# Choosing the tokens of eight experts: one search for all ahead of them, or one for the first and the others in steps between matmuls

## The chip, the cores and the metric

The kernel runs on one core of a Trainium2 chip. The metric is the device time of one execution in microseconds (us). Before the change it is 1625.28, the median of three runs from 1625.16 to 1626.9. Engines are named as in the profile: PE (TensorE matmul), PEld (its weight load), DVE (VectorE), ACT (ScalarE), POOL (GpSimd), SP (SyncE).

## The reference

The input is 4 rows of 1024 tokens with 256 values each, float32. Two layers follow, each an attention part and a feed-forward part around layer norms and residual sums. Only the last part matters here, a mixture of eight experts in which each expert chooses its tokens:

```python
n = b * l                                   # 4096 tokens
k = min(max(int(n * C / e), 1), n)          # 4096 * 2 / 8 = 1024 per expert
S = jax.nn.sigmoid(xt @ Wg).T               # scores, 8 x 4096
G, I = jax.lax.top_k(S, k)
ex = xt[I]
hid = jax.nn.gelu(jnp.einsum('ekh,ehf->ekf', ex, W1) + b1[:, None, :], approximate=False)
out = (jnp.einsum('ekf,efh->ekh', hid, W2) + b2[:, None, :]) * G[..., None]
new_x = jnp.zeros_like(xt).at[I.reshape(-1)].add(out.reshape(-1, h))
```

W1 is 8 x 256 x 1024 and W2 8 x 1024 x 256. A layer norm of new_x is added to the tokens at the end.

## The kernel before, in words

The tokens lie in SBUF in eight blocks of 512, each in four tiles of 128. The first layer runs block by block, the second layer's attention row by row; PE, DVE and ACT issue in the order in which the program is written (a hand-made schedule), POOL and SP in the order of the framework's scheduler. POOL too is ordered by hand from the seventh expert on.

**End of the attention.** For the last two tiles of 128 tokens, `close` returns the function `at_once` (L1249). It projects the attention output, adds the residual, does three layer norms one after the other on DVE with a `pow` on POOL in each, stores the normalized tokens in `tok_d` (L1190), transposes them (`turn_gating`, L1203) and computes their gate logits (`gate`, L1216), which it adds to the tile `logits` (L1233). `logits` has 128 partitions, one per pair of a token segment and an expert (16 segments of 256 tokens), and 256 columns. `keep_busy` (L203) issues matmuls whose result nobody reads.

**Search.** After that, in the stage that begins at L1434, `sc` becomes the sigmoid of all logits (L1468 to L1471). It is also transposed and stored beside the token rows, eight DMAs of 32-byte rows (L1486). Each expert's threshold, the 1024th largest score, is then found bit by bit for all experts at once: 15 rounds (L1497) of two bits. A round compares all scores with three values, each in an operation that also counts (L1501), adds up the counts over the 16 segments of the expert with a matmul by the 0/1 matrix `same_b` (L1505), and keeps the largest value with a count of at least 1024 (L1516, L1520). The next values to try are that value with two more bits (L1509).

**Lists.** From the threshold follow, for all experts in the same operations, a mask, the ties that still have room, the place of each chosen token in its expert's list (two scans, L1548 and L1552), a transpose to tokens, and the two halves of the place, `hi` (which chunk of 128) and `lo` (where in it), L1556 to L1564. What is left is done per expert by the class `List` (L1571): `chunks` and `places` build 0/1 matrices on DVE, `collect` multiplies them on PE in 32 small bf16 matmuls into the PSUM tile `parts`, ACT copies this to `listed`, and `gather` makes the token numbers `idx` with one more matmul and has POOL fetch eight chunks of 128 token rows from `tok_d` into `got` with indirect DMAs (L1628).

**Experts.** `feed_forward(u)` (L1805) does 512 tokens, half an expert; u runs from 0 to 15, two units (QPE = 2) per expert. Its first part has FC = 8 pairs of float32 matmuls `ph` (L1819), each followed by a Gelu on ACT; its second part has four output tiles of 128 tokens, `py` (L1842), which DVE scales and POOL adds to `acc_d` in DRAM with an indirect DMA (L1861). The tokens of the next unit are transposed on PE (`turn`, L1790) after the second and third output tile. Unit 0 does its first part in two halves of 256 tokens. While an expert's first unit runs, the next expert's `chunks` and `places` are issued among the ph matmuls, its four `collect` groups between ph and py, and its `gather` after the first output tile. Two sets of expert weights are loaded at a time, from SP.

Of the kernel before, what the change touches and what calls it, by code (L numbers as in the profile page):

```python
# [18 lines left out]
P = 128  # L19
D = 256  # L20
# [27 lines left out]
NROUND = 15  # L48
# [23 lines left out]
def kernel(  # L72
# [130 lines left out]
    def keep_busy(bank, n):  # L203

        for _ in range(n):
            nc.tensor.matmul(
                bank, lhsT=same_b, rhs=same_b.unsqueeze(1).to_broadcast([P, 4, P]), start=True, stop=True
            )
# [18 lines left out]
    with ExitStack() as st1:  # L227
# [183 lines left out]
        def later_counts():  # L411
            r = {}

            def count_int(name, shape, pattern, per_partition, tag=None):
                n_i = const.tile(shape, I32, tag=tag or name, name=name, bufs=3 if tag else 1)
                nc.gpsimd.iota(n_i, pattern=pattern, base=0, channel_multiplier=per_partition)
                return n_i

            def count(name, shape, pattern, per_partition, dtype):
                n_i = count_int(f"{name}_i", shape, pattern, per_partition, "whole")  # L420
                r[name] = const.tile(shape, dtype, name=name)
                nc.gpsimd.tensor_copy(r[name], n_i)
# [3 lines left out]
            count("count_p", [P, P], [[1, P]], 0, BF16)  # L426
            count("count_c", [P, NC], [[1, NC]], 0, BF16)
            count("count_t", [P, SEG // P, SEGB, B], [[1, SEG // P], [SEG // P, SEGB], [KT, B]], 0, BF16)
            r["count_t"] = r["count_t"].rearrange("p k z b -> p (k z b)")
            count("in_tile", [P, 1], [[0, 1]], 1, F32)  # L430
            r["row_i"] = count_int("row_i", [P, 1], [[0, 1]], 1)
            r["bits0"] = count_int("bits0", [P, 4], [[1, 4]], 0)
            r["expert_i"] = count_int("expert_i", [P, P], [[1, P]], -1, "whole")
            r["column_i"] = count_int("column_i", [P, P], [[1, P]], 0, "whole")
# [7 lines left out]
        def later_constants(r):  # L442
# [13 lines left out]


            def segment(name, n, p_i):

                row = const.tile([P, n], I32, tag="whole", name=f"{name}_row", bufs=3)  # L460
                nc.vector.tensor_scalar(row, p_i, 3, B - 1, ALU.logical_shift_right, ALU.bitwise_and)
                nc.vector.tensor_scalar(p_i, p_i, 5, None, ALU.logical_shift_right)
                n_f = const.tile([P, n], F32, name=name)
                nc.vector.scalar_tensor_tensor(n_f, row, float(SEGB), p_i, ALU.mult, ALU.add)
                return n_f

            expert_i = r["expert_i"]
            nc.vector.tensor_scalar(expert_i, expert_i, NE - 1, None, ALU.bitwise_and)

            same_b = const.tile([P, P], BF16, name="same_b")  # L470
            nc.vector.tensor_scalar(same_b, expert_i, 0.0, None, ALU.is_equal)
            earlier_b = const.tile([P, P], BF16, name="earlier_b")
            nc.vector.scalar_tensor_tensor(
                earlier_b, segment("seg_m", P, r["column_i"]), segment("seg_k", 1, r["row_i"]), same_b,
                ALU.is_gt, ALU.mult,
            )

            bits = const.tile([P, NROUND, 4], I32, name="bits")
            for n in range(NROUND):
                nc.vector.tensor_scalar(  # L480
                    bits[:, n, :], r["bits0"], 2 * (NROUND - 1 - n), None, ALU.logical_shift_left
                )

            counts = []
            for i in range(2):
                count_i = const.tile([P, 4], BF16, name=f"counts{i}")
                nc.vector.memset(count_i, float(SEG))
                counts.append(count_i)
# [4 lines left out]
            return mb1, strip, same_b, earlier_b, bits, counts, fold  # L493
# [468 lines left out]
        for t in range(NB):  # L962
# [6 lines left out]
            elif t == 1:  # L969
                mb1, strip, same_b, earlier_b, bits, counts, fold = later_constants(whole)  # L970
# [69 lines left out]
    spare = const.tile([P, 1], F32, name="spare")  # L1040
    with ExitStack() as st3:
# [96 lines left out]
        def close(t, h, oT, tiles, at_end):  # L1138
# [77 lines left out]
            def gate():  # L1216
# [15 lines left out]
                rows = slice(32 * (z0 + us[0]), 32 * (z0 + us[-1] + 1))  # L1232
                nc.vector.tensor_tensor(logits[rows, :], logits[rows, :], pg[rows, :], ALU.add)  # L1233
# [15 lines left out]
            def at_once(by_weight, back):  # L1249
# [7 lines left out]
                keep_busy(idle, 4)  # L1257
# [4 lines left out]
                keep_busy(idle, 34)  # L1262
                for i, pt in pts:
                    nc.vector.tensor_tensor(y[:, i, :], pt, h[:, i, :], ALU.add)
# [13 lines left out]
                gate()  # L1278
# [155 lines left out]
    with ExitStack() as st4:  # L1434
# [5 lines left out]
        parts = parts_ps.tile([P, P + NC], F32, name="parts")  # L1440
        nc.vector.memset(parts, 0.0)
# [14 lines left out]

        hi = keep.tile([P, NE, NTILE], BF16, name="hi")
        lo = keep.tile([P, NE, NTILE], BF16, name="lo")  # L1460
        each = keep.tile([P, P, NTILE], BF16, name="each")
        with ExitStack() as sa:
            wk = sa.enter_context(tc.tile_pool(name="gate", bufs=2))
            w1 = sa.enter_context(tc.tile_pool(name="pick", bufs=1))
            ps = sa.enter_context(tc.tile_pool(name="gate_ps", bufs=2, space=PSUM))

            sc = w1.tile([P, SEG], F32, name="sc")
            nc.vector.tensor_scalar(sc, logits, -87.0, None, ALU.max)  # L1468
            nc.scalar.activation(sc, sc, AF.Exp, scale=-1.0)
            nc.vector.tensor_scalar(sc, sc, 1.0, None, ALU.add)  # L1470
            nc.vector.reciprocal(sc, sc)  # L1471
            idle = ps.tile([P, TB], F32, tag="idle", name="idle", bufs=1)
            keep_busy(idle, 13)

            def by_token(src, name):
                pt = ps.tile([P, SEG // P, NSEG * NE], F32, tag="tp", name=name)
                for k in range(SEG // P):
                    nc.tensor.transpose(pt[:, k, :], src[:, k * P : (k + 1) * P], ident)
                return pt

            scores_t = w1.tile([P, SEG // P, SEGB, B, NE], F32, name="scores_t")
            nc.scalar.copy(scores_t.rearrange("p k z b e -> p k (z b e)"), by_token(sc, "scoreT"))
            rows_d = tok_d.rearrange("(b z k p) d -> k z p b d", b=B, z=SEGB, p=P)
            for k in range(SEG // P):
                for z in range(SEGB):
                    nc.sync.dma_start(rows_d[k, z][:, :, D : D + NE], scores_t[:, k, z])  # L1486
            nc.scalar.copy(each, count_p.unsqueeze(2).to_broadcast([P, P, NTILE]))

            nc.scalar.activation(spare, sc[:, 0:1], AF.Gelu)

            thr = w1.tile([P, 1], F32, name="thr")
            tried = bits[:, 0, :].bitcast(F32)
            for r in range(NROUND):  # L1497
                n = counts[r % 2]
                for k in range(1, 4):
                    ge = wk.tile([P, SEG], F32, tag="ge", name="ge")  # L1500
# [70 lines left out]
        class List:  # L1571


            def __init__(self, e):
                self.e, self.at = e, {}
# [351 lines left out]
```

## Time and profile before

| what | us |
|---|---|
| median of the runs | 1625.28 |
| profiled execution | 1625.33 |
| its span | 1623.5 |
| last attention product ends, about | 1075 |
| sigmoid done, first comparison | 1093.27 |
| threshold known, mask begins | 1122.99 |
| `hi`, `lo` ready, `which` begins | 1130.42 |
| `idx` of expert 0 begins | 1135.37 |
| first `ph` matmul | 1141.76 |
| last `py` matmul ends, about | 1613 |

Times of instructions are counted from the span's start. In a row of a timeline the first number is the start, the second the length, then the engine, the line, the operation, its output and inputs. A row with x32 stands for 32 instructions. In rows by stage the busy time of each engine follows the stretch and its length. A float32 matmul of the program shows as two PE instructions.

### The profile page before, as it was taken

To read this page: it belongs to the slowest core of one execution; us is meant where nothing else is said; L and a number is where in the kernel's file an instruction comes from. 1 tells how busy PE (TensorE), PEld (TensorE's weight loads), DVE (VectorE), ACT (ScalarE), POOL (GpSimd) and SP (SyncE) were. 2 spreads that over 40 slices of the span, in tenths; PEclk is the share of its full clock that TensorE was granted. 3 is DMA by queue.
4 is the path that set the end of the run, shared out by engine and by line. 5 is a ranking of instruction groups with operands and counts; after the bars stand their busy time and mean duration, and the time that the engine had idled before them with its cause. 6 is when DMAs were issued, how large, how long until landed. Compare 5 with 4: busy or idle time off the path is not lost.

```text
span 1623.5 us, 23583 instructions
## 1 busy us (share of the span) xinstructions
PE 1562.3 (96%) x9270; PEld 797.6 (49%) x9270; DVE 904.9 (56%) x2080; ACT 647.6 (40%) x1115; POOL 402.0 (25%) x436
## 2 busy tenths in 40 slices
PE   7999999999999999999999999983999999999997
PEld 3666666666322223232323224541757667566574
DVE  5555565664657787878787787767211212222145
ACT  3344444544544545454544455641221121211233
POOL 4122232222201011111101010110424324324555
PEclk9999999999999999999999999996999999999999
DMA  8300000000000000101010100031233233233355
GB/s 205 121 1 1 1 1 1 0 1 1 1 1 1 11 31 7 34 1 40 1 40 1 36 4 27 28 129 30 57 75 70 66 75 72 66 75 88 67 146 140
DMA packets 70090, 71.22 MB, mean 44 GB/s; under 512 B 23613, under 2 KB 62938, under 8 KB 69850
## 3 DMA queue, kind: packets, MB, share of 16 engines
q1 hardware_dynamic: 56096, 47.01, 9.4%
q0 software_dynamic: 13008, 21.77, 7.4%
q8 instruction: 73, 1.20, 0.3%
q10 hardware_dynamic: 874, 0.93, 0.2%
q14 instruction: 39, 0.32, 0.1%
HBM read 41.74 MB, written 27.95 MB: 43 GB/s over the span
## 4 chain that ended last, share of the span: by engine, by line
PE 92%; DVE 3%; issue 2%; POOL 1%; ACT 1%; DMA 0%; POOLq 0%; SPq 0%; ACTq 0%; DVEq 0%
PE sc L1303 17%; PE po L1329 16%; PE ph L1819 13%; PE py L1842 13%; PE py L799 4%; PE pg L691 4%; PE pv L707 3%; PE ph L855 2%; PE po L771 2%; PE pt L1145 2%; PE pv L380 2%; PE pq L356 2%; PE pq L876 2%; PE po L775 2%; PE pk L356 2%
## 5 line engine op out<-in xcount | busy, mean ns | idle before, releaser
L1312 ACT ACTIVATE w<-sc 128x512 f32<-128x512 f32 x512 | 277.9, 594 | 218.5 <-PE sc L1303 101.7
L1317 DVE TENSOR_SCALAR w<-sc 128x1024 f32<-128x1024 f32 x240 | 293.2, 1222 | 99.2 <-PE sc L1303 71.1
L1303 PE MATMUL sc<-qT,kT 32*128 32x512 f32 (+1 forms) x2304 | 294.7, 586 | 1.5 <-ACT w L1312 0.8
L1329 PE MATMUL po<-w,vaug 128*17 128x512 f32 (+1 forms) x2304 | 276.1, 550 | 1.0 <-ACT w L1315 0.3
L1842 PE MATMUL py<-w,hid 128*128 128x256 f32 x1024 | 230.1, 380 | 0.0
L1826 ACT ACTIVATE hid<-ph,mb 128x512 f32<-128x512 f32 (+1 forms) x136 | 90.1, 662 | 344.4 <-PE ph L1819 343.7
L1819 PE MATMUL ph<-xT,w 128*128 128x512 f32 (+1 forms) x544 | 222.8, 567 | 0.7 <-DVE xT L1803 0.7
L1842 PEld LDWEIGHTS py<-w,hid 128*128 128x128 f32 x1024 | 191.1, 190 | 32.0 <-issue 7.0
L1303 PEld LDWEIGHTS sc<-qT,kT 32*128 32x128 f32 x2304 | 94.4, 183 | 173.9 <-issue 157.9
L1819 PEld LDWEIGHTS ph<-xT,w 128*128 128x128 f32 x544 | 103.2, 190 | 111.1 <-issue 107.6
L1329 PEld LDWEIGHTS po<-w,vaug 128*17 128x17 f32 x2304 | 44.8, 95 | 191.5 <-issue 157.5
L1861 POOL DMA_INDIRECT acc_d<-y,idx x56 | 88.2, 1574 | 156.1 <-issue 127.0
L1628 POOL DMA_INDIRECT got<-tok_d,idx x64 | 65.9, 1030 | 152.3 <-DVE idx L1618 135.2
L1859 DVE TENSOR_TENSOR y<-py,mb 128x256 f32<-128x256 f32 x56 | 23.4, 419 | 142.3 <-PE py L1842 135.9
L1803 DVE COPY xT<-tp 128x512 f32<-128x512 f32 (+1 forms) x34 | 22.3, 660 | 91.6 <-PE tp L1798 91.6
L1067 POOL TENSOR_TENSOR rsg<-veg,mhalf 128x1 f32<-128x1 f32 x30 | 16.7, 555 | 205.0 <-DVE veg L1066 205.0
L691 PE MATMUL pg<-nT,wh 128*128 128x512 f32 x128 | 60.8, 607 | 1.5 <-ACT nT L630 1.5
L799 PE MATMUL py<-wo,oT 128*128 128x256 f32 x256 | 61.9, 385 | 0.0
L707 PE MATMUL pv<-wh,nT 128*128 128x512 f32 x128 | 59.7, 592 | 0.0
L1618 DVE CAST idx<-parts 128x8 int32<-128x8 f32 x8 | 1.3, 167 | 101.8 <-PE parts L1616 101.8
L799 PEld LDWEIGHTS py<-wo,oT 128*128 128x128 f32 x256 | 47.3, 190 | 17.2 <-issue 9.4
L572 POOL TENSOR_TENSOR x<-x,y 128x1024 f32<-128x1024 f32 x14 | 32.9, 2351 | 73.3 <-ACT y L561 73.3
(295 smaller groups left out, 1933.3 us busy)
## 6 DMA issues: line engine op xcount, KB each, us to landing
w<-in_L_ffn_W_dram SPq DMA_DIRECT2D x16, 1024.0 KB, 5.2
x<-in_L_attn_x_dram SPq DMA_DIRECT2D x8, 512.0 KB, 4.0
acc_d<-logits SPq DMA_DIRECT2D x8, 512.0 KB, 5.1
tok_d<-hg SPq DMA_DIRECT2D x32, 128.0 KB, 1.7
x_d<-x SPq DMA_DIRECT2D x7, 512.0 KB, 2.9
back_w<-acc_d SPq DMA_DIRECT2D x6, 512.0 KB
out_dram<-x SPq DMA_DIRECT2D x20, 128.0 KB, 1.7
out_dram<-back_w POOLq DMA_DIRECT2D x4, 512.0 KB
```

The costliest lines, as they stand in the source:

```text
L691: nc.tensor.matmul(pg, lhsT=wh[:, c, HID + e * P : HID + (e + 1) * P], rhs=d["nT"][:, c, :], start=(c == 0), stop=(c == DC - 1),)
L707: nc.tensor.matmul(pv, lhsT=d["nT"][:, c, i * P : (i + 1) * P], rhs=wh[:, c, 0:HID], start=(c == 0), stop=(c == DC - 1),)
L799: nc.tensor.matmul(py, lhsT=d["oT"][:, e, :], rhs=wo[:, e, :], start=(e == 0), stop=(e == EC - 1))
L1303: nc.tensor.matmul(sc[:, m * n : (m + 1) * n], lhsT=row["kT"][t][rows, r, (kt + m) * P : (kt + m + 1) * P], rhs=row["qT"][rows, t, q0 : q0 ...
L1312: nc.scalar.activation(w[:, j, :], sc, AF.Relu)
L1317: nc.vector.tensor_scalar(w[:, 2:4, :], pair, 0.0, None, ALU.max)
L1329: nc.tensor.matmul(po[32 * j : 32 * j + HD + 1, weighed(halves, r)], lhsT=row["v"][:, kt + m, HQ * t + 2 * j + r, :], rhs=w[:, j, m * n : ...
L1628: return nc.gpsimd.indirect_dma_start(out=dst, out_offset=None, in_=rows[:, :], in_offset=self.at_chunk(c), bounds_check=NT - 1, oob_is_er ...
L1819: nc.tensor.matmul(ph, lhsT=w1[:, c, f * P : (f + 1) * P], rhs=xT[u][:, c, h * n : (h + 1) * n], start=(c == 0), stop=(c == DC - 1),)
L1826: nc.scalar.activation(hid[:, f, h * n : (h + 1) * n], ph, AF.Gelu, bias=mb1[:, e * FC + f : e * FC + f + 1])
L1842: nc.tensor.matmul(py, lhsT=hid[:, f, i * P : (i + 1) * P], rhs=w2[:, f, :], start=(f == 0), stop=(f == FC - 1),)
L1861: scatter = nc.gpsimd.indirect_dma_start(out=acc_d[:, :], out_offset=lists[e].at_chunk(k), in_=y, in_offset=None, bounds_check=NT - 1, oob ...
```

## The change

The 15 rounds for all experts are replaced by `Search` objects: one for expert 0, one for expert 1, one for 2 and 3, one for 4 to 7. Scores now lie by tokens: `score_t` has 128 partitions (token in its tile) and 32 x 8 columns (tile, expert), in the memory of `logits`. A round takes three bits: seven values are compared with the expert's 32 columns in one `tensor_tensor` per expert, into a bf16 tile of 7 x 32, and one `tensor_reduce` adds up the 32. There are ten rounds. The matmul that adds up over partitions is by `all_b`, all ones. Only expert 0's search forms the next values for all outcomes ahead of the counts (`grown`); the others choose first and put the bits in afterwards.

Ranks are done per expert too (`sort`, `rank`), on 32 columns: two matmuls (by `all_b` and the triangular `upto_b`), two scans and some small operations.

Ahead of the experts stand expert 0's search and list. While its first rows are fetched, three steps of expert 1's search are issued. All other steps are in `agenda`, in order, each with a planned time and the first unit at which it may be issued. `go_on_with_lists` is called after every pair of ph matmuls, with 1.75 us (0.87 in unit 0), and after every output tile, with 2.3 us; it issues at most one step, when at most 0.3 us of the steps before are planned to be left.

`at_once` now transposes the logits that are known and computes their sigmoid and stores it beside its own chain; those of the last 256 tokens follow by themselves. Score stores to `tok_d` are two DMAs.

```diff
-NROUND = 15
+NBITS, NPER = 30, 3
+NVAL = 2**NPER
...
             def at_once(by_weight, back):
...
-                keep_busy(idle, 4)
+                tokens = side([P, SEG // P, P], "tokens")
+                for k in range(SEG // P):
+                    nc.tensor.transpose(tokens[:, k, :], logits[:, k * P : (k + 1) * P], ident)
+                keep_busy(idle, 3)
                 by_weight()
                 back()
...
+                for k in range(SEG // P):
+
+                    nc.vector.tensor_scalar(
+                        score_t.rearrange("p (b z k) e -> p k z b e", b=B, k=SEG // P)[:, k],
+                        tokens[:, k, :].rearrange("p (z b e) -> p z b e", b=B, e=NE),
+                        -87.0, None, ALU.max,
+                    )
+                known = score_t[:, 0 : NTILE - SEG // P]
+                nc.scalar.activation(known, known, AF.Exp, scale=-1.0)
...
                 turn_gating(tiles[0])
-                gate()
+                nc.vector.tensor_scalar(known, known, 1.0, None, ALU.add)
+                nc.vector.reciprocal(known, known)
+                score_rows = tok_d.rearrange("(j p) d -> p j d", p=P)[:, :, D : D + NE]
+                nc.sync.dma_start(score_rows[:, 0 : NTILE - SEG // P], known)
+
+                pg, rows = gate()
+                last_logits = wk.tile([P, SEG], F32, tag="y", name="last_logits")
+                nc.vector.tensor_copy(last_logits[rows, :], pg[rows, :])
+                tokens = side([P, SEG // P, 32], "tokens")
+                for k in range(SEG // P):
+                    nc.tensor.transpose(tokens[:, k, :], last_logits[rows, k * P : (k + 1) * P], ident[rows, rows])
+                new = score_t[:, NTILE - SEG // P : NTILE]
+                nc.vector.tensor_scalar(new, tokens[:, :, 32 - NE : 32], -87.0, None, ALU.max)
+                nc.scalar.activation(new, new, AF.Exp, scale=-1.0)
+                nc.vector.tensor_scalar(new, new, 1.0, None, ALU.add)
+                nc.vector.reciprocal(new, new)
+                nc.sync.dma_start(score_rows[:, NTILE - SEG // P : NTILE], new)
...
+            def compare(self, r):
+                g = len(self.es)
+                ge = wk.tile([P, NE // 2, NVAL - 1, NTILE], BF16, tag="ge", name="ge", bufs=1)
+                shape = [P, NVAL - 1, NTILE]
+                for i, e in enumerate(self.es):
+                    nc.vector.tensor_tensor(
+                        ge[:, i],
+                        score_t[:, :, e].unsqueeze(1).to_broadcast(shape),
+                        self.tried[:, i, 1:].unsqueeze(2).to_broadcast(shape),
+                        ALU.is_ge,
+                    )
+                with nc.allow_low_precision(reason="whole numbers up to 32"):
+                    nc.vector.tensor_reduce(self.counts[:, r % 2, :, 1:], ge[:, 0:g], AX.X, ALU.add)
+
+            def tick(self, r):
+
+                g, v = len(self.es), NVAL
+                pn = parts[:, sums_at : sums_at + g * v]
+                counts = self.counts[:, r % 2].rearrange("p g v -> p (g v)")
+                nc.tensor.matmul(pn, lhsT=all_b, rhs=counts, start=True, stop=True)
...
+                    if self.es == (0,):
...
+                        nc.vector.tensor_tensor(
+                            grown.bitcast(I32),
...
+                        nc.vector.scalar_tensor_tensor(
+                            kept, pn.to_broadcast([P, v, v]), float(TOPK), grown, ALU.is_ge, ALU.mult
+                        )
+                        nc.vector.tensor_reduce(tried[:, 0], kept, AX.X, ALU.max)
+                    else:
...
+                        nc.vector.scalar_tensor_tensor(kept, pn, float(TOPK), self.tried, ALU.is_ge, ALU.mult)
+                        best = wk.tile([P, g], F32, tag="best_g", name="best")
+                        nc.vector.tensor_reduce(best, kept, AX.X, ALU.max)
+                        nc.vector.tensor_tensor(
+                            tried.bitcast(I32),
+                            best.bitcast(I32).unsqueeze(2).to_broadcast([P, g, v]),
+                            now.unsqueeze(1).to_broadcast([P, g, v]),
+                            ALU.bitwise_or,
+                        )
+                    self.tried = tried
+                    self.compare(r + 1)
...
+            def steps(self, behind=0):
+
+                spent = 0.15 + 0.6 * len(self.es)
+                return [
+                    (spent, behind, lambda: self.compare(0)),
+                    *((spent + 0.85, behind, lambda r=r: self.tick(r)) for r in range(NBITS // NPER)),
+                ]
...
+            def rank(self):
+
+                for n, which in enumerate((all_b, upto_b)):
+                    nc.tensor.matmul(
+                        pre[:, n].rearrange("p v j -> p (v j)"),
+                        lhsT=which,
+                        rhs=self.kinds.rearrange("p v j -> p (v j)"),
+                        start=True,
+                        stop=True,
+                    )
...
+            def steps(self):
+
+                behind = max(QPE * self.e - 3, 0)
+                return [
+                    (0.5, behind, self.sort),
+                    (2.6, behind, self.rank),
+                    (1.2, behind, self.chunks),
+                    (1.4, behind, lambda: (self.places(0), self.places(1))),
+                    (1.4, behind, lambda: (self.places(2), self.collect(0), self.places(3), self.collect(1))),
+                    (0.3, behind, lambda: (self.collect(2), self.collect(3))),
+
+                    (0.3, behind + 1, self.gather),
+                ]
...
-                if not u:
+                if not u and not h:
                     for c in range(DC):
-                        turn(0, c, h)
+                        turn(0, c, 0)
                 for f in range(FC):
+                    if not u and not h and f in (FC - 4, FC - 3):
+                        turn(0, f - FC + 4, 1)
...
+                    if u or h or f not in (FC - 5, FC - 4, FC - 3):
+                        go_on_with_lists(u, 1.75 if u else 0.87)
...
-                if i == 0 and coming is not None:
-                    coming.gather()
-                if i in (1, 2) and u + 1 < NE * QPE:
+                if u == 1:
+                    if i == 2:
+                        for c in range(DC):
+                            turn(u + 1, c)
+                elif i in (1, 2) and u + 1 < NE * QPE:
                     turn(u + 1, i - 1)
...
+                go_on_with_lists(u, 2.3)
...
+        searches = [Search(0), Search(1), Search(2, 3), Search(4, 5, 6, 7)]
+        agenda = []
+        for search in searches[1:]:
+            agenda.extend(search.steps())
+            for e in search.es:
+                agenda.extend(lists[e].steps())
+        left = [0.0]
+
+        def go_on_with_lists(u, time):
+            left[0] = max(left[0] - time, 0.0)
+            if agenda and left[0] < 0.3 and agenda[0][1] <= u:
+                spent, _, step = agenda.pop(0)
+                left[0] += spent
+                step()
+
         first = ps.tile([P, TB], F32, tag="mm", name="idle", bufs=3)
-        keep_busy(first, 15)
+        for n, (_, _, step) in enumerate(searches[0].steps() + lists[0].steps()):
+            step()
+            if n == 0:
+                nc.vector.memset(parts[:, 0 : P + NC], 0.0)
+            if step == lists[0].rank:
+                keep_busy(first, 8)
+        for _ in range(3):
+            agenda.pop(0)[2]()
+            keep_busy(first, 4)
```

## The prediction

> **What bounds the kernel now.** I read the page's totals first, then the busy time by stage, then the chain of work and the instructions in order of time inside the one stage where TensorE isn't full.
>
> ```profile
> PE 1562.3 (96%) x9270; PEld 797.6 (49%) x9270; DVE 904.9 (56%) x2080; ACT 647.6 (40%) x1115; POOL 402.0 (25%) x436
> ...
> 1060.00:1110.00 50.00, 31.99 (x289) 15.96 (x281) 35.59 (x135) 17.40 (x25) 4.50 (x7) 0.87 0.42 130
> 1110.00:1150.00 40.00, 24.33 (x129) 13.59 (x130) 21.62 (x88) 4.71 (x10) 8.42 (x8) 0.78 0.10 28
> 1150.00:1200.00 50.00, 50.00 (x232) 36.85 (x232) 11.42 (x26) 9.56 (x17) 17.34 (x14) 1.00 0.26 56
> 1200.00:1300.00 100.00, 100.00 (x408) 64.17 (x407) 21.24 (x49) 19.79 (x30) 35.86 (x29) 1.00 0.33 71
> ```
>
> Columns after the stretch: its length, then busy us of PE, PEld, DVE, ACT, POOL, the granted clock, DMA. PE is the bound nearly everywhere, the experts' stage included (100.00 of 100.00, DVE at 21), but not between about 1075 and 1142 us. There VectorE and short round trips set the time. One of the 15 rounds of the search, from the chain that ended last:
>
> ```profile
> 1119.04 1.30 DVE ge L1501 x6
> 1120.34 0.05 issue
> 1120.38 0.20 PE pn L1505
> 1120.61 0.19 DVE kept L1516
> 1120.82 0.18 DVE tried L1520
> 1121.02 1.30 DVE ge L1501 x6
> ```
>
> The round repeats after 1.98 us (1119.04 to 1121.02): three compare-and-count passes in 1.30, a matmul of counts, two small VectorE steps. Two dependent VectorE steps stand 0.03 apart beyond their length. So whatever shortens this stage moves the end, and whatever adds PE work after 1142 moves it back.
>
> What PE pays for one small bf16 matmul between float32 ones shows at the list's gather matmul:
>
> ```profile
> 1187.43 7.07 PE L1842 MATMUL py<-w,hid 128*128 128x256 f32 x32
> ...
> 1217.89 3.72 PE L1842 MATMUL py<-w,hid 128*128 128x256 f32 x16
> 1221.45 0.17 PE L1616 MATMUL parts<-fold,listed 128*128 128x8 bf16 x1
> 1221.47 3.70 PE L1842 MATMUL py<-w,hid 128*128 128x256 f32 x16
> 1225.01 0.60 PE L1798 MATMUL tp<-ident,got 128*128 128x128 f32 x4
> ```
>
> Two py blocks with it: 1217.89 to 1225.01 = 7.12 us; without it 1187.43 to 1194.34 (the next transpose) = 6.91. So 0.21 us, though the matmul has 8 columns.
>
> **What the Trainium skill says.** "VectorE: DVE Perf Modes", the perf-mode tier table: float32 tensor_tensor and every tensor_reduce run at one element a cycle. The trace agrees for the first: x<-x,back_w of 128x1024 took 1.225 us and upto<-upto,mask of 128x256 0.42, so 1.05 ns an element and 0.152 fixed. For the reduce it has only 16 elements, 0.17 us. "TensorE: Matmul & The Clock Gate", Part 1: the array drops to half clock when idle and needs some 3.4 us of work to come back. Here the granted clock is 0.50 from 1098 to 1126, and 13 matmuls begun at 1124.01 bring it to 1.00 after 1127.4. "SBUF — State Buffer", Who interferes with whom: a VectorE instruction with two SBUF inputs contends with a GpSimd instruction that reads SBUF. Before, VectorE is idle during the first gather, so no row here shows it.
>
> **The change part by part.** The profiled execution took 1625.33 us, span 1623.5 and 1.8 around it; the median is 1625.28, the same within 0.1.
>
> *Scores.* Before, from the last logits add (1089.53) to the first comparison (1093.27): 3.74 us, 1.75 of it the reciprocal of 256 columns. After, all but the last two of the 32 token tiles are done earlier. Their two clamps lie in VectorE's 0.79 wait for pt (1077.07 to 1077.86; two 128-column PSUM reads, about 0.29 each), their add and reciprocal (0.28 + 1.65) in its 2.37 wait for pg (from 1087.2): cost nothing, with 0.2 to 0.4 to spare; without cover about 2.5. On the path stay a copy 0.43, two small transposes 0.25, clamp 0.17, exp 0.22, add 0.15, reciprocal of 16 columns 0.25 (den has that shape and time), and six gaps of 0.04: 1.7. **Gain 2.05.** The extra PE transposes stand where one filler matmul goes. SP's score stores change from 8 issues to 2 with the same 32-byte rows (6.3 us to land before); weights of 3 MB may stand before or behind them on that queue. DMA was quiet from 1104, and the first reader comes at about 1115, so neither order costs.
>
> *Search.* A round of the first expert: kept and its maximum over 64 elements, 0.22 each (0.17 for 16 elements, plus 48 more at 1.05 ns); the comparison 7x32 = 224 elements, 0.152 + 0.235 = 0.39; the sum over the same 224, 0.39; four gaps of 0.03, issue 0.05, matmul 0.20, gap 0.03: 1.62. The or of 64 integers fits in the matmul's wait. A strided read is no extra: lo<-part, 256 elements at such a stride, took 0.39. Ten rounds: nine of 1.62, the first comparison 0.85 and a last 0.7: 16.1 (15.5 to 17, the reduce being unseen at this size). Before: 1093.27 to 1122.99 = 29.7. **Gain 13.6.**
>
> *List of expert 0.* Before, thr to which: 1122.99 to 1130.42 = 7.4, over 256 columns and with transposes. After: two compares of 32 columns 0.3, matmul 0.3, two scans 0.4 (256 took 0.68), then nine steps of 0.15 to 0.22, two of them overlapping: about 2.8. **Gain 4.6.** From which to idx (5.1) and to the first ph (6.2) the operations stay. Three steps of expert 1's search go into the gather's wait: some 4.1 us of VectorE work in the 5.7 before the first xT copy, so no cost unless they slow POOL's descriptors (0 to 4, taken 0). ACT's each copy and Gelu table (3.6 + 1.3 in before, 1094 to 1099) come earlier and are over long before listed needs ACT at about 1114. The memset of parts, 0.17, moves into the first matmul's wait of 0.28: nothing, 0.17 uncovered. POOL's memsets of the counts are new; the queue is idle from 1086.4 and they are due at 1091.6: nothing, about 0.5 each (its shortest tensor steps take 0.26 to 0.55) if late. Eight fillers behind rank take 8 x 0.43 = 3.4 at half clock, over before the first collect is ready.
>
> *Start of expert 0.* The second half's transposes go between ph matmuls, so PE's 0.39 wait for xT at 1149.76 goes. **Gain 0.4.** Sum of gains 20.65.
>
> *What comes back.* Seven experts' searches and ranks now stand in PE's queue in the full stage. 3 x 10 counts less the 2 issued early = 28 matmuls; at 0.2 (from the 0.21 above) 5.6. Seven ranks of two matmuls, 0.3: 2.1. Collect in two groups where it was one: seven more interruptions, 1.4. **Cost 9.1.** The bounds are 0.1 apiece (a transpose amid py costs 0.11) and 0.3: 4.5 to 14.
>
> Does a count matmul wait for VectorE? Behind it are all ph and py. Walking the agenda: in the first unit a step goes every second slot, 2 x 0.87 of ph and 0.2; VectorE's chain for one expert is 3 x 0.2 + 0.85 and gaps, 1.6. For two experts 2.4 against 3.5 or more. For four experts the comparison is 4 x 0.39 and the sum 896 elements, 1.1; with the small steps 3.5 against 3.7. Just enough, so 0; if the chain is 20% slower, 0.5 on each of seven ticks, 3.5. All lists are out in unit 12, and list 1's gather in unit 1, 15 us ahead of its transposes, on a POOL queue that issues the first unit's scatters earlier. Y evictions wait behind a step for up to 3.5 us, with two py banks: no cost.
>
> Sum: -20.65 + 9.1 = -11.5 us. **1625.3 - 11.5 = 1613.8.** In L0 the constants change a few operations beside a full PE: nothing.
>
> **The rivals.**
> - *Cheap insertions*, 0.1 each: PE prefetches weights (PEld is 64% busy in the stage) and hides all but the matmul. 1625.3 - 20.65 + 4.5 = 1609. Against: the 0.21 is measured in this very place.
> - *Wait in place of wait.* VectorE's new work meets POOL's descriptors of the first gather (+3), the four-expert ticks hold PE (+3.5), or PE starts expert 0 at half clock (+2 to 3): one or two of them, about 1619. For it: the thin margin, 8 fillers instead of 25; against: DVE is 21% busy in the stage.
> - *Slower.* Each insertion drains PE's pipeline and holds the float32 weights behind it. Place: the 42 insertions counted above (28 counts, 7 rank pairs, 7 collect groups). From 20.65/42 = 0.49 us each nothing is left, from 0.57 it is slower by over 0.2%; at 0.7 it costs 29.4 and ends at 1634. For it: each comes alone, after a wait on VectorE's semaphore, which gather's doesn't test; against: gather's 0.21.
>
> **How the numbers follow.** Forecast 1613.8, chance 0.58 (1611 to 1617). Cheap insertions 0.22. Wait in place of wait 0.15, some of it within 0.2% of before (3.3 us, about what a measurement here can tell from no change). Slower 0.03, and 0.02 for what I don't see. Range 1608 to 1619.5. Faster by over 0.2% 0.93, within 0.04, slower 0.03.
>
> **What would show it.** Right: tried to tried 1.6 us; first comparison near 1091.2; threshold near 1107; first ph near 1121.5; first ph to the end some 9 us longer than before (481.8), with parts and pre rows of 0.2 each. Wrong: the new sum far above 0.39 us; PE waiting for DVE at the counts in the experts' stage; granted clock below 1.00 after the first ph; got fetches longer than 1.02 us.

## The result and the profile after

The changed kernel takes 1616.98 us, the median of five runs from 1616.53 to 1618.01; the kernel before, run beside it, 1625.49 (five runs, 1625.16 to 1626.9). The ratio is 0.9946, 95% interval 0.9932 to 0.9961: 8.5 us less, where 11.5 were forecast. The profiled execution is the slowest of the five: 1618.01 us, span 1616.2.

The same rows of totals and stages as before (columns: length, busy us of PE, PEld, DVE, ACT, POOL, granted clock, DMA):

```profile
PE 1562.5 (97%) x9275; PEld 793.4 (49%) x9275; DVE 976.7 (60%) x2259; ACT 649.2 (40%) x1116; POOL 404.8 (25%) x440
...
1060.00:1110.00 50.00, 30.53 (x302) 16.00 (x299) 37.52 (x114) 20.10 (x28) 4.88 (x12) 0.82 0.43 130
1110.00:1150.00 40.00, 36.38 (x190) 25.28 (x190) 24.29 (x83) 9.12 (x18) 10.67 (x10) 0.92 0.13 31
1150.00:1200.00 50.00, 49.69 (x203) 29.98 (x202) 30.52 (x85) 10.30 (x16) 18.85 (x15) 1.00 0.37 83
1200.00:1300.00 100.00, 97.31 (x412) 62.11 (x412) 61.82 (x158) 17.99 (x28) 35.93 (x28) 1.00 0.31 67
```

Two things are to be seen. From 1110 to 1150 PE is busy for 36.38 us instead of 24.33: the experts begin earlier. But from 1200 to 1300, where PE was busy for 100.00 of 100.00, it is now busy for 97.31, with DVE at 61.82 instead of 21.24. That stage was full and has a hole.

One round of expert 0's search, in order of time:

```profile
1103.02 0.17 PE L1513 MATMUL parts<-counts,all_b 128*128 128x8 bf16 x1 [1.58 <-DVE counts L1506]
...
1103.22 0.23 DVE L1528 SCALAR_TENSOR_TENSOR kept<-parts,grown 128x64 f32<-128x64 f32 x1
1103.48 0.22 DVE L1531 TENSOR_REDUCE tried<-kept 128x8 f32<-128x64 f32 x1
1103.74 0.55 DVE L1499 TENSOR_TENSOR ge<-logits,tried 128x224 bf16<-128x224 f32 x1
1104.32 0.39 DVE L1506 TENSOR_REDUCE counts<-ge 128x7 bf16<-128x224 bf16 x1
...
1104.77 0.17 PE L1513 MATMUL parts<-counts,all_b 128*128 128x8 bf16 x1 [1.58 <-DVE counts L1506]
```

The round repeats after 1.75 us (1103.02 to 1104.77), not after the forecast 1.62. The sum, kept and the maximum took what was forecast (0.39, 0.22, 0.22). The comparison, with as many elements as the sum, took 0.55 instead of 0.39.

What an inserted count costs, between py blocks of the first unit:

```profile
1139.99 0.17 PE L1513 MATMUL parts<-counts,all_b 128*128 128x8 bf16 x1
1140.02 3.70 PE L1883 MATMUL py<-w,hid 128*128 128x256 f32 x16
1143.56 0.17 PE L1513 MATMUL parts<-counts,all_b 128*128 128x8 bf16 x1
1143.59 3.70 PE L1883 MATMUL py<-w,hid 128*128 128x256 f32 x16
1147.12 0.60 PE L1844 MATMUL tp<-ident,got 128*128 128x128 f32 x4
```

From 1139.99 to 1147.12 two blocks and two counts, one before each, take 7.13 us. Two blocks alone took 6.91 (1187.43 to 1194.34 before). That is 0.22 for two counts, 0.11 each, where 0.2 was forecast: each count takes 0.03 until the next block starts, and that block is some 0.08 longer. The prediction's 0.21 was read from one gather matmul between two blocks, and the first of those blocks itself came right behind a list's 32 collect matmuls, so that two interruptions lie in it. An experiment below measures the count by itself.

Where PE waits at counts from 1122 to 1600 us (us in all, times, longest), the place in the four-expert search where it does, and VectorE there:

```profile
PE parts L1513 <- DVE counts L1506: 3.0, 7, 1.1
```

```profile
1279.68 0.18 PE L1513 MATMUL parts<-counts,all_b 128*128 128x32 bf16 x1
1279.71 3.68 PE L1866 MATMUL ph<-xT,w 128*128 128x512 f32 x8
1284.50 0.18 PE L1513 MATMUL parts<-counts,all_b 128*128 128x32 bf16 x1 [1.11 <-DVE counts L1506]
1284.52 3.68 PE L1866 MATMUL ph<-xT,w 128*128 128x512 f32 x8
1288.52 0.18 PE L1513 MATMUL parts<-counts,all_b 128*128 128x32 bf16 x1 [0.32 <-DVE counts L1506]
```

```profile
1281.37 1.95 DVE L1499 TENSOR_TENSOR ge<-logits,tried 128x224 bf16<-128x224 f32 x4
1283.35 1.09 DVE L1506 TENSOR_REDUCE counts<-ge 128x28 bf16<-128x896 bf16 x1
1284.71 0.19 DVE L1534 SCALAR_TENSOR_TENSOR kept<-parts,tried 128x32 f32<-128x32 f32 x1 [0.27 <-PE parts L1513]
```

From count to count it is 4.02 us (1284.50 to 1288.52), set by VectorE: four comparisons in 1.95 (1.56 were forecast), the sum 1.09 (as forecast), three small steps. PE's own work in between, two ph pairs and the count, would be over some 0.4 earlier, and everything behind the count stands still for that long.

The longest wait, the 1.11, has a second cause. VectorE takes two steps for the last output tile of the unit before it turns to the count of 1279.68:

```profile
1279.88 0.42 DVE L1902 TENSOR_TENSOR y<-py,mb 128x256 f32<-128x256 f32 x1 [1.07 <-PE parts L1513]
1280.34 0.45 DVE L1903 TENSOR_SCALAR y<-y,got 128x256 f32<-128x256 f32 x1
```

Only at 1280.72 does `kept` begin, 0.86 after the count's end. The prediction had asked whether an output tile waits behind a step of the search, not whether the search waits behind a tile.

The span divides so, in the two profiled executions:

| stretch | before | after | change | forecast |
|---|---|---|---|---|
| start to the last logits copy or add | 1089.53 | 1091.19 | +1.65 | 0 |
| to the first comparison | 3.74 | 1.78 | -1.96 | -2.05 |
| to the threshold | 29.72 | 17.63 | -12.09 | -13.6 |
| to `which` | 7.43 | 2.86 | -4.57 | -4.6 |
| to the first ph | 11.34 | 11.36 | +0.02 | 0 |
| first ph to the end of the last py | 471.15 | 480.88 | +9.73 | +8.7 (9.1 - 0.4) |
| rest | 10.6 | 10.5 | -0.1 | 0 |

They add up to -7.3, the difference of the spans. The +1.65 of the first line has two parts. 1.28 lie at the very start of the kernel and aren't the change's: the eight `psim` matmuls there begin at 20.60 us before, at 21.88 after, and at 20.08 to 21.71 in the kernels below, which share the changed kernel's code up to there. PE's half clock lasts longer or shorter from one execution to the next: the traces' first record of full clock is at 14.8 us before, 17.2 after and 13.7 in the run that reaches `psim` at 20.08. The other 0.37 come at about 1029 us, in the attention of the last row. From `psim` to the `turned` at 1066.10 it is 1045.50 us before, and to the same `turned` 1045.84 to 1045.88 in all nine profiles of the changed kernel and its variants, so this part isn't scatter; no run here shows where it comes from. Without the late start the change is worth -8.6 in the profile, as in the runs (8.5).

### The profile page after: what moved, and what is told of

It reads as the page before. It is cut to its first block, busy times and chain, and to the rows that moved or that the text cites. A ratio compares the mean times of both kernels' runs of the same rounds, so it can differ in the third digit from the quotient of the medians.

```text
span 1616.2 us, 23781 instructions
## 1 busy us (share of the span) xinstructions
PE 1562.5 (97%) x9275; PEld 793.4 (49%) x9275; DVE 976.7 (60%) x2259; ACT 649.2 (40%) x1116; POOL 404.8 (25%) x440
## 5 line engine op out<-in xcount | busy, mean ns | idle before, releaser
L1866 PE MATMUL ph<-xT,w 128*128 128x512 f32 (+1 forms) x544 | 230.2, 574 | 0.3 <-DVE xT L1849 0.3
L1866 PEld LDWEIGHTS ph<-xT,w 128*128 128x128 f32 x544 | 99.8, 190 | 109.7 <-issue 100.6
L776 PEld LDWEIGHTS py<-wo,oT 128*128 128x128 f32 x256 | 47.3, 190 | 17.2 <-issue 9.6
L841 ACT ACTIVATE hid<-ph,vec 128x512 f32<-128x512 f32 x64 | 39.8, 685 | 25.3 <-PE ph L832 25.1
```

The lines of the kernel that those rows point to most:

```text
L776: nc.tensor.matmul(py, lhsT=d["oT"][:, e, :], rhs=wo[:, e, :], start=(e == 0), stop=(e == EC - 1))
L1866: nc.tensor.matmul(ph, lhsT=w1[:, c, f * P : (f + 1) * P], rhs=xT[u][:, c, h * n : (h + 1) * n], start=(c == 0), stop=(c == DC - 1),)
```

## The experiments

Theory: the whole loss against the forecast has one root, the comparison's strided read. The scores lie by tokens with the eight experts side by side, so a comparison reads an expert's 32 scores 32 bytes apart, and pays for it. That lengthens the search by 1.6 us, and the four-expert rounds past the time that they were given, so that PE waits. The insertions, on the other hand, cost about half of what was forecast, which hides most of it. Rivals: the comparison is slow for its broadcast operands or its bf16 output, whatever the step; the insertions cost the 0.21 forecast and the waits are cheap because they overlap the pipeline's refill; the stage ahead needs no fillers. In the expectations, A is the theory that follows from these readings, and B and C are its rivals. The kernel before took 1625.49, 1625.75 and 1626.12 us in the three series of runs, so a difference of half a microsecond between runs of different series says nothing.

**Scores by expert** (e1_rows). A copy of the scores in the memory of `wgp`, free by then, holds each expert's 32 scores next to each other; comparison and sort read it. A POOL copy of 30 tiles and one of two are added.

```diff
+    score_e = wgp.rearrange("p c z n -> p (c z n)").rearrange("p (e j) -> p e j", e=NE)
...
+                nc.gpsimd.tensor_copy(score_e[:, :, 0 : NTILE - SEG // P].rearrange("p e j -> p j e"), known)
...
-                nc.vector.reciprocal(new, new)
+                last_e = score_e[:, :, NTILE - SEG // P : NTILE].rearrange("p e j -> p j e")
+                nc.vector.reciprocal(last_e, new)
+                nc.gpsimd.tensor_copy(new, last_e)
...
-                        score_t[:, :, e].unsqueeze(1).to_broadcast(shape),
+                        score_e[:, e, :].unsqueeze(1).to_broadcast(shape),
```

> The changed kernel, but the comparisons (and the two compares of sort) read the scores from a copy in which each expert's 32 columns lie side by side; POOL makes the copy beside other work. Theory A: the comparison of 7x32 took 0.55 us, and 0.467 each back to back, because one input steps by 32 bytes; side by side it takes 0.39. Then a round of the first expert falls from 1.745 to 1.58 us, ten of them by 1.65, the four-expert ticks fit their time and the 3 to 4 us that TensorE waits for counts go: 1617.0 - 5.4 = 1611.6. Rival B: two float32 inputs of which one is broadcast cost two cycles an element whatever the stride: the comparison stays at 0.55 and the time within 1 us of 1617.

Measured: 1611.54 us (five runs, 1611.45 to 1612.43), ratio to before 0.9912 [0.9899, 0.9926]; 5.4 less than the changed kernel. The comparison's group from 1090 to 1600 us (after the bar: busy us, mean ns), first in the changed kernel, then with scores by expert, and what then still waits at a count:

```profile
L1499 DVE TENSOR_TENSOR ge<-logits,tried 128x224 bf16<-128x224 f32 x72 | 36.8, 553 | 1.2
```

```profile
L1503 DVE TENSOR_TENSOR ge<-wgp,tried 128x224 bf16<-128x224 f32 x72 | 25.0, 388 | 1.2
```

```profile
PE parts L1517 <- DVE counts L1510: 0.4, 1, 0.4
```

The same shape and types, broadcast as before, in 388 ns instead of 553. The round is 1.58 us (tried at 1094.22 to tried at 1095.80), and first comparison to threshold 16.04 (1092.57 to 1108.61), the forecast 16.1. Four comparisons in a row take 1.29 instead of 1.95. The waits fall from 3.0 us to 0.4, what is left being the one behind an output tile, and first ph to last py from 480.88 to 477.33. So 1.6 of the 5.4 come from the search ahead and 3.55 from the experts; the rest is within the scatter of the runs. The broadcast and the bf16 output are not what costs.

**The same with steps of 8 and of 16 bytes** (e6_step8, e7_step16). Copy and memory are those of the run before, but two or four experts stay side by side.

```diff
+    score_e = wgp.rearrange("p c z n -> p (c z n)").rearrange("p (h j l) -> p h j l", l=2, j=NTILE)
...
-                        score_t[:, :, e].unsqueeze(1).to_broadcast(shape),
+                        score_e[:, e // 2, :, e % 2].unsqueeze(1).to_broadcast(shape),
```

(With 4 in place of each 2 for 16 bytes.)

> As the run with each expert's scores side by side, but two experts' scores alternate in the copy, so that the comparison's scores step by 8 bytes. If any step other than one costs a second cycle, the comparison takes 0.55 us again and the time is near 1617; if only steps beyond 16 bytes do, it takes 0.39 and the time is near 1611.5.

> The same with four experts' scores alternating, a step of 16 bytes. If a step that leaves a 16-byte line with every element costs a second cycle, the comparison takes 0.55 us and the time is near 1617, with the step of 8 bytes between (a new line every second element: 0.39 to 0.47) or unharmed; if only the 32 bytes of the changed kernel cost, 0.39 and 1611.5.

Measured: 1611.78 (1611.23 to 1612.15), ratio 0.9911 [0.9896, 0.9926], with 8 bytes; 1616.95 (1616.17 to 1617.91), ratio 0.9944 [0.9931, 0.9958], with 16. The comparison with 8, then with 16 bytes:

```profile
L1506 DVE TENSOR_TENSOR ge<-wgp,tried 128x224 bf16<-128x224 f32 x72 | 24.9, 387 | 1.2
```

```profile
L1506 DVE TENSOR_TENSOR ge<-wgp,tried 128x224 bf16<-128x224 f32 x72 | 36.6, 550 | 1.2
```

4 and 8 bytes take 388 and 387 ns, 16 and 32 bytes 550 and 553. The run with 16 bytes is also the control of the first one: the same copy in the same memory, and nothing gained. So it is the step, and the edge lies between 8 and 16 bytes. The 16-byte line of the second expectation is from the Trainium skill: the page "SBUF — State Buffer", Door 1, has a remark on 16-byte lines, each of which needs at least two hits for full bandwidth. The runs agree: two float32 scores of an expert fall into 16 bytes with a step of 8, one with a step of 16. The page gives no price; here it is 0.166 us for 224 elements, 0.74 ns an element.

**Time given to the four-expert rounds** (e3_plan). The plan's duration for a step of that search is raised by 0.7 us, and with it the distance between its counts; the slow comparison stays.

```diff
-                spent = 0.15 + 0.6 * len(self.es)
+                spent = 0.15 + 0.6 * len(self.es) + (0.7 if len(self.es) == 4 else 0.0)
```

> The changed kernel with one number of the plan changed: a step of the four-expert search counts as 0.7 us longer, so that it is issued every third ph pair, not every second, and later output tiles. Same operations. Theory A: the counts then find VectorE done, the waits in units 4 and 5 go (four of 0.43, one of 1.23, and those of the later ticks: 3.4 in all): 1613.6. Rival B: the waits are no loss, since the work behind them would wait elsewhere: 1617.

Measured: 1613.05 (1612.98 to 1614.12), ratio 0.9922 [0.9908, 0.9936]; 3.9 less than the changed kernel. The same place on PE, and what waits at counts in the experts:

```profile
1280.08 0.18 PE L1513 MATMUL parts<-counts,all_b 128*128 128x32 bf16 x1
1280.11 5.40 PE L1866 MATMUL ph<-xT,w 128*128 128x512 f32 x12
1285.34 0.18 PE L1513 MATMUL parts<-counts,all_b 128*128 128x32 bf16 x1
1285.37 5.40 PE L1866 MATMUL ph<-xT,w 128*128 128x512 f32 x12
```

```profile
PE parts L1513 <- DVE counts L1506: 0.3, 1, 0.3
```

A count now comes after three ph pairs, 5.26 us, and finds its numbers ready. The counts themselves are as many as before. First ph to last py falls to 477.23, as with scores by expert. So the waits cost 3.7 (by the stage) to 3.9 us (by the medians), 3.55 with scores by expert, though only 2.6 to 2.7 of the 3.0 of idle time are gone from the trace: they are not hidden by a refill that is due anyway. What makes them cost about 1 us more than their idle time is not shown.

**72 counts that nobody needs** (e2_lone). After each ph pair and each output tile of six units in which the agenda issues little or nothing, one matmul by `all_b`, 8 columns, that is meant to wait for nothing.

```diff
+        def lone(u):
+            if u in (8, 10, 12, 13, 14, 15):
+                nc.tensor.matmul(parts[:, sums_at : sums_at + NC], lhsT=all_b, rhs=fold, start=True, stop=True)
```

> The changed kernel plus 72 lone matmuls of 8 bf16 columns by all_b, whose result nobody reads and which wait for nothing: after each pair of ph matmuls and each output tile of units 8, 10, 12, 13, 14 and 15. It measures the price of one insertion into the full stage. Theory A: 0.115 us (two py or ph blocks around a count stand that much further apart), 72 of them 8.3: 1625.3. Rival B, the forecast's price of 0.21: 15.1, so 1632. Rival C, nothing, TensorE prefetches the weights and hides it all: 1617 to 1619 (the bare matmul, 0.03 each).

Measured: 1625.52 (13 runs, 1624.75 to 1626.28), ratio to before 0.9997 [0.9989, 1.0006]; 8.54 more than the changed kernel. That is 0.119 for each. In the trace:

```profile
1436.13 0.17 PE L1853 MATMUL parts<-fold,all_b 128*128 128x8 bf16 x1 [0.35 <-DVE idx L1664]
1436.15 1.96 PE L1870 MATMUL ph<-xT,w 128*128 128x512 f32 x4
1437.95 0.17 PE L1853 MATMUL parts<-fold,all_b 128*128 128x8 bf16 x1
1437.98 1.96 PE L1870 MATMUL ph<-xT,w 128*128 128x512 f32 x4
1439.78 0.17 PE L1853 MATMUL parts<-fold,all_b 128*128 128x8 bf16 x1
```

The distance is 1.83 us; a ph pair alone takes 1.74 (four of them 6.96 in the trace of the best version, 1152.32 to 1159.28), so 0.09 for the count here. Three of the 72 wait for `idx`, as the first row shows, 1.1 us together; without them 0.10 for each. The forecast's 0.2 was twice too much, and its rival's 0.1 was right.

**Four experts at once ahead of the experts** (e4_ahead). Both searches, of experts 0 to 3 and 4 to 7, stand ahead of expert 0's list; 12 fillers take the place of the early steps.

```diff
-        searches = [Search(0), Search(1), Search(2, 3), Search(4, 5, 6, 7)]
+        searches = [Search(0, 1, 2, 3), Search(4, 5, 6, 7)]
...
-        for n, (_, _, step) in enumerate(searches[0].steps() + lists[0].steps()):
+        for n, (_, _, step) in enumerate(searches[0].steps() + searches[1].steps() + lists[0].steps()):
```

> The other part of the change alone: seven values in one operation and a sum, by tokens, but the thresholds of all eight experts ahead of the experts' stage, as two searches of four one after the other; the lists stay in the agenda. Theory A: a round of four experts takes the 4.02 us that it took in the experts' stage where TensorE waited for it, twenty of them 80 against 17.6 for the first expert alone; back come the 28 counts (3.2) and the waits (3.8) in the stage: 1617 + 63 - 7 = 1673. So the new round alone would be slower than before by some 48 us. Rival B: the round by itself is the gain and the interleaving adds little: below 1630.

Measured: 1672.08 (1671.75 to 1672.3), ratio 1.0283 [1.0268, 1.0299]: 46 us slower than before the change. A round:

```profile
1111.77 0.19 PE L1513 MATMUL parts<-counts,all_b 128*128 128x32 bf16 x1 [3.81 <-DVE counts L1506]
...
1112.66 1.93 DVE L1499 TENSOR_TENSOR ge<-logits,tried 128x224 bf16<-128x224 f32 x4
1114.62 1.09 DVE L1506 TENSOR_REDUCE counts<-ge 128x28 bf16<-128x896 bf16 x1
1115.77 0.19 PE L1513 MATMUL parts<-counts,all_b 128*128 128x32 bf16 x1 [3.81 <-DVE counts L1506]
```

4.00 us a round, 20 rounds. So comparing seven values over tokens isn't in itself cheaper than before: for all experts it would be 80 us where the old search took 29.7. The gain comes from leaving seven experts' rounds to the time in which PE has other work; PE there pays only for counts, ranks, further collect groups and waits.

**No fillers** (e5_nofill). The 24 matmuls that nobody reads, 8 behind rank and 16 up to the first transposes, are left out.

```diff
-                    keep_busy(first, 4)
...
-            if step == lists[0].rank:
-                keep_busy(first, 8)
...
-            keep_busy(first, 4)
```

> The changed kernel without the 24 filler matmuls after the first expert's rank (8), after the three early steps (4 each) and after the first transposed tile (4). Theory A: TensorE is then at half clock when expert 0 begins, since it has done little for 30 us but the 2.4 us of collect; the first 3 to 4 us of ph run at half speed, and collect, at half clock, takes up to 1 us longer: 1617.0 + 2.5 = 1619.5, with a granted clock below 1 after the first ph. Rival B: collect and the transposes raise the clock by themselves: 1617.

Measured: 1618.57 (1618.07 to 1625.58), ratio 0.9955 [0.9941, 0.9968]; 1.6 more than the changed kernel. Its profiled execution is the one of 1625.58: in the last unit ACT stands behind a POOL step for 7.83 us, and PE with it, which no other profile here shows; only what lies far ahead of that is read. By stretches of 4 us around the first ph, in the changed kernel and then without fillers:

```profile
1116.00:1120.00 4.00, 3.18 (x33) 1.11 (x26) 2.22 (x7) 1.55 (x2) 0.54 (x1) 0.97 0.00 0
1120.00:1124.00 4.00, 2.82 (x14) 0.94 (x12) 2.61 (x9) 0.00 (x0) 3.08 (x4) 1.00 0.25 68
1124.00:1128.00 4.00, 3.70 (x18) 2.86 (x19) 2.34 (x8) 1.13 (x3) 3.08 (x4) 1.00 0.38 103
```

```profile
1116.00:1120.00 4.00, 0.64 (x7) 0.21 (x3) 2.45 (x8) 1.55 (x2) 1.71 (x2) 0.93 0.02 3
1120.00:1124.00 4.00, 1.91 (x6) 1.19 (x6) 2.29 (x7) 0.00 (x0) 3.09 (x4) 0.50 0.36 98
1124.00:1128.00 4.00, 4.00 (x15) 3.04 (x14) 1.47 (x6) 1.02 (x3) 3.09 (x4) 0.69 0.39 103
```

The collect, which ends at 1117.62 and at 1116.15, takes 2.43 us in both, where the expectation had it slower without fillers, and in the first stretch the clock is near full in both (0.97 and 0.93). But without fillers PE is busy for only 0.64 us there, the clock falls back to 0.50 in the next, and the first ph matmuls, at 1123.49, run at half clock: unit 0 takes 31.57 us instead of 30.23. The fillers are worth what they were put there for, 1.3 us in unit 0 and 1.6 by the medians, and the prediction was right to see full clock at the first ph. Whether the 8 behind rank are needed for that, or only the 16 behind the collect, isn't shown.

**Scores by expert and one collect group per list** (e8_group), the version that the other runs point to.

```diff
-                    (1.4, behind, lambda: (self.places(2), self.collect(0), self.places(3), self.collect(1))),
-                    (0.3, behind, lambda: (self.collect(2), self.collect(3))),
+                    (1.4, behind, lambda: (self.places(2), self.places(3))),
+                    (0.3, behind, lambda: [self.collect(part) for part in range(4)]),
```

> The kernel with each expert's scores side by side, and the 32 collect matmuls of a list in one group where they were two groups of 16 between ph matmuls: seven insertions fewer. Theory A: an insertion costs 0.115 us: 1611.5 - 0.8 = 1610.7. Rival B, the forecast's 0.2: 1610.1. Rival C: it is the 32 matmuls that cost, not the place: 1611.5.

Measured: 1610.25 (1609.77 to 1610.61), ratio 0.9903 [0.9888, 0.9918], the fastest here: 6.7 less than the changed kernel, 15.9 less than the one before in the same series. The collect stands in one piece:

```profile
1152.32 7.03 PE L1870 MATMUL ph<-xT,w 128*128 128x512 f32 x16
1159.28 2.01 PE L1654 MATMUL parts<-at,pair 128*16 128x128 bf16 x32
1161.22 1.98 PE L1870 MATMUL ph<-xT,w 128*128 128x512 f32 x4
```

Against the run with 8-byte steps, which differs in nothing else that costs and ran in the same series (1611.78), it is 1.5 us faster: 0.22 for each of seven interruptions left out (0.29 by first ph to last py in the two profiles, 477.27 and 475.21). Against the run with scores by expert it is 1.3. The forecast's 0.2 for a second collect group holds, if anything as too little; it is the lone counts that are cheaper.

## Why the prediction was nearly right, step by step

- *Scores, 2.05.* Right: 1.96. The early half of the sigmoid and the order of stores and weights on SP cost nothing that shows. Expert 0's weights went ahead of the score stores and expert 1's behind them, the last store's issue took 3.93 us, and PE's first wait for fetched rows was 0.2.
- *Search, 13.6.* The mechanism was right, one term mis-sized: 12.09 came. Of the round's terms, the comparison's 0.39 was 0.55. The step that failed is "A strided read is no extra", drawn from `lo<-part`, a cast of 256 elements with one input. Nor did the line show that the cast's own step was free: its 0.39 is below the 0.42 of a two-input operation of as many elements, but right ahead of it an operation of the same 256 elements with one input, at a step of 4 bytes, took 0.29 (both lines stand below this list). No run here varied the cast's step, so that stays open. The price list that the forecast took, the Trainium skill, "VectorE: DVE Perf Modes", the perf-mode tier table, with one element a cycle, holds for the step of 4 and 8 bytes (0.39) and not for 16 and 32. For the reduction, whose size had not been seen, it was right: 0.39 for 224 elements, 1.09 for 896.
- *List of expert 0, 4.6.* Right: 4.57.
- *which to the first ph, 0.* Right: 11.36 against 11.34. Three of expert 1's steps beside POOL's descriptors cost nothing: after the first, of 1.31 in both, the fetches took 1.01 to 1.13 us where they took 1.01 to 1.02, with 0.3 between them as before.
- *ACT's tables.* Earlier, as told, and at no cost, but with something left out. The copy of `each` and the Gelu table came even before the last sigmoid's exp (1080.46 and 1084.07), so that the tables were changed twice more, 1.28 us each. The first change ended at 1091.35, 0.87 ahead of its use, the second 6.6 ahead.
- *Start of expert 0, 0.4.* Right: PE's only wait for `xT` is the 0.30 ahead of the first ph.
- *Insertions, 9.1.* Too much: the runs without waits lose 6.1 from first ph to last py (477.2 - 471.15), 6.5 with the 0.4 just named. 28 counts at 0.10 to 0.12 are 3, seven second collect groups at 0.22 to 0.29 are 1.5 to 2; the rest, 1.5 to 2, is put down to the ranks and what is left of waits (0.3), which no run measures apart. The step that failed is the 0.2 for a count, taken from the gather's matmul.
- *Waits at the counts, 0.* Wrong: 3.6 to 3.9. The forecast had walked to the right place, with 3.5 us of VectorE's chain against 3.7, and had priced its failure at 3.5. The chain took 4.02, mostly by the four comparisons' 1.95 instead of 1.56, and PE's slot was 3.6. Where a unit ends, the steps for its last output tile came on top. A cost of zero on a margin of 0.2, resting on a duration that no row had shown, was the weak choice.

The cast, and the operation ahead of it, in the kernel before:

```profile
1129.61 0.29 DVE L1563 TENSOR_SCALAR part<-place 128x256 int32<-128x256 int32 x1
1129.93 0.39 DVE L1564 CAST lo<-part 128x256 bf16<-128x256 int32 x1
```

The sum: -11.55 as forecast, +1.5 in the search, +0.1 in the scores, +0.4 in the last row's attention, +3.7 of waits and -2.8 of insertions and small things is -8.6, what the profile shows without its late start. So the time fell into the forecast's range by luck as well: two errors of some 3 us in the experts' stage, which the forecast had not set against each other, nearly cancel. By its own list it was half cheap insertions and half wait in place of wait. Of that rival's three causes one came true, the rounds of four experts; contention with POOL and a start at half clock did not. Slower than before, from 0.49 us for an insertion, was far off.

Of the signs it named, tried to tried came out at 1.75 for 1.6, the threshold at 1110.6 for 1107 (1.65 of that from ahead of the search), first ph to the end at +9.6 for +9; the second sign of being wrong, PE waiting for VectorE at counts, is the one that appeared. (One fetch of 1.13 was above the 1.02 of the fourth, and cost nothing.)

## What to carry to other kernels

When work is moved behind a full engine, what counts is no longer how long it takes but whether each result is ready when the engine comes to it: here 0.17 us more in a comparison cost 1.6 us where it lay on the path, and 3.6 us where a margin of 0.2 was to cover four of them. A price for a strided operand should come from the same kind of operation seen with and without the step, and an interruption's price from one that stands between the same two neighbours. Where a plan holds the durations, correct the plan or the data's layout before the algorithm: each recovered nearly all the waits.

## What was not expected of the hardware

- A float32 comparison with two SBUF inputs, 128 x 224: 388 ns with scores 4 bytes apart, 387 with 8, 550 with 16, 553 with 32.
- A lone bf16 matmul of 8 columns amid float32 matmuls with weights of their own costs PE 0.09 to 0.12 us, though it shows as 0.17 and brings its own weights.
- The clock, once granted (0.93 of the stretch after the collect), was back at 0.50 within 4 us in which PE was busy for 0.64. The Trainium skill, "TensorE: Matmul & The Clock Gate", Part 1, says this of an idle window of some 3.4 us, and the trace agrees, with PE not wholly idle.
- Executions of code that is the same up to there differ by 1.8 us in the first 22 us alone (20.08 to 21.88 for the start of the same matmuls), with full clock first recorded at 13.7 and 17.2 us.
